# The second layer's bias of a two-layer MLP: from four small matrix products a window to one VectorE addition a pair of tiles, with a new order of the steady group

## The chip, the cores and the metric

The kernel runs on one core of one Trainium2 chip. A core has five engines that run their own instruction streams side by side and wait for each other by semaphores: TensorE (PE in the profile; its weight loads are listed as PEld), VectorE (DVE), ScalarE (ACT), GpSimd (POOL) and SyncE (SP, which here only issues DMAs). The metric is the device time of one execution in microseconds (us), as the median of several runs. Lower is better.

## The reference, cut to what matters

```python
def _mlp_ln(s, W1, b1, W2, b2, g, b):
    h = jax.nn.silu(s @ W1 + b1) @ W2 + b2
    return _ln(h, g, b)                          # (x - m) * rsqrt(v + EPS) * g + b
h = _ln(x, pw_g[pathway_ids], pw_b[pathway_ids])
h = _ln(h, cp_g[compartment_ids], cp_b[compartment_ids])
t = _ln(x, tm_g[time_steps], tm_b[time_steps])
m, n, r = x + (a normed MLP of a conditioning vector, one row a batch)   # three such
s = _ln(x, ms_g[scale_type], ms_b[scale_type])
cat = concatenate([w[0]*h, w[1]*t, w[2]*m, w[3]*n, w[4]*r, w[5]*s], axis=-1)
return x + _mlp_ln(cat, int_W1, int_b1, int_W2, int_b2, int_g, int_be)
```

x is 16 x 512 x 512 in float32, so there are 8192 tokens of 512 features. What is changed here is where `int_b2`, the bias of the second layer of the last MLP, is added.

## The kernel before, in words

**Tiling.** The 8192 tokens are walked in 16 windows of 512 tokens. A window is four tiles of 128 tokens (numbered 0 to 3), and two tiles make a pair (0 and 1 are pair 0, 2 and 3 are pair 1). Tokens are gathered by index from memory, so that a window shares its small tables.

**The order of the work** is written out by hand in three lists of short names: `ORDER` for the start, `WINDOW` for the steady group that is run once for each window (`run(WINDOW, w)`, L1408), and `LAST` for the last window. A name is a kind of step, a window and a number: `c` is the window at hand, `n` the next one, `m` the one after it, `p` the one before. Each engine runs its own steps in the order in which they stand in the list, so that the list fixes five queues at once. Pieces of three windows lie beside each other in one group.

**The steps that matter here**, with the lines under which the profile shows them:

- `lV` (layer1, L371): product of a tile's normed x with the window's own 512 x 512 matrix; four a window, 8 recorded matmuls each (a float32 matmul is recorded as two).
- `m7.c.p.k` (half_product, L419): two tiles' remaining first-layer products by seven products of half size (Strassen's scheme in Winograd's form), k from 1 to 7 for pair p, 8 recorded matmuls each. Sums of their inputs are made on VectorE: `u1` to `u4` (token_sum, L400, L402, L404, L406) write into the transposed tiles cX, cH and a tile ss. What comes out is added up on VectorE by `r1`, `r2`, `r3`, `r5` (L428 to L436) and `ha` (L439).
- `hs` (L442, ScalarE) is the SiLU, `tz` (L169, VectorE) turns a tile into rZ, and `sZ` (spread_row, L177) moves rZ to cZ by DMAs that SyncE issues, four for each of four rows. `tx`, `th`, `tv` and `sX`, `sH`, `sV` do the same for x, h and the normed x of the window. All these DMAs stand in SyncE's one queue.
- `zs` (z_sums, L499 to L505, GpSimd) makes the input sums of the second layer's seven products: `zs.p.0` to `zs.p.3` for pair 0, `zs.p.4` to `zs.p.7` for pair 1.
- `q7.p.q.k` (seventh, L522): the second layer of the window before, again as seven products for each pair q, 4 recorded matmuls each. They run in two banks of PSUM for a pair, called ab and ed (pq_0a, pq_0b, pq_1a, pq_1b in the profile).
- `kf`, `ku` (L531, L533, L544, ScalarE) copy from these banks to the result yb; `sf`, `sl` (L538, L540, L549, L551, VectorE) add what belongs to it. After `sl.p.1` both rows of tiles of pair 0 are finished, after `sl.p.3` those of pair 1.
- `lq` (L587, ScalarE) sums the squares of a finished tile, `lv` (L595) and `lp` (L600, GpSimd) make the inverse deviation, `lb` (L608, L609, VectorE) scales and adds x, `po` (L613, GpSimd) writes the tile out by an indirect DMA. `gx` gathers a later window's x into the buffer that this frees.
- `f1` (L314, L315), `f2` (L351), `fs`, `fv`, `fp`, `fn`, `th` are the chain of h; `bd` (L233) rebuilds a window's matrix where its group of tables changes, under a condition read from memory.

**The bias before.** `bias_parts` (L470) splits the row of b2 into three bfloat16 parts once, in b2r. In `seventh`, the products k = 1 and k = 5 are preceded by a small product of a constant with that row (L520, 96 rows x 256 columns in bfloat16), which starts the accumulation, so that the bias is in PSUM before the true product is added. All results that the seven products make up contain product 1 or 5 in the right way, so four small products a window do it. The first window and the last one go through `layer2` and `last_add` (L582), which add the row on VectorE.

Of the kernel before, what the change touches and what calls it, by code (L numbers as in the profile page):

```python
# [15 lines left out]
P = 128  # L16
# [9 lines left out]
WINDOW = """
    ha.p.2 lV.c.1 hs.p.2 sh.c.1 tz.p.3 gc.c.2 tz.p.2 sp.c.3 gc.c.3 f1.c.2 fs.c.2 f1.c.3 m7.c.1.1 m7.c.0.1 lV.c.0
    xs.n.0 fs.c.3 sh.c.0 bd.c.3 lV.c.3 fv.c.2 f2.c.2 f2.c.3 sZ.p.2 ga.c.0 sZ.p.0 xs.n.1 q7.p.1.1 fp.c.2 fv.c.3 fn.c.2
    q7.p.0.1 sZ.p.1 fp.c.3 q7.p.0.2 fn.c.3 sZ.p.3 sp.c.2 th.c.2 th.c.3 xs.n.2 zs.p.0 zs.p.1 bd.c.2 q7.p.0.5 kf.p.0
    q7.p.1.2 sH.c.0 sf.p.0 gh.n.0 zs.p.2 tx.n.3 kf.p.1 tx.n.0 q7.p.0.6 xs.n.3 zs.p.4 q7.p.0.7 ku.p.0 zs.p.5 q7.p.1.5  # L30
    zs.p.3 xe.n kf.p.2 tx.n.1 xp.n ga.c.1 sf.p.1 sH.c.3 tx.n.2 xm.n kf.p.3 q7.p.0.3 q7.p.1.7 sf.p.2 nv.n.3 q7.p.0.4
    sl.p.0 zs.p.6 nv.n.1 ga.c.2 zs.p.7 sh.c.3 tv.n.3 tv.n.1 r1.c.0 gc.n.0 sf.p.3 sl.p.1 nv.n.2 tv.n.2 m7.c.0.2 nv.n.0
    ga.c.3 sH.c.2 sH.c.1 lq.p.0 gh.n.1 tv.n.0 q7.p.1.3 lq.p.1 q7.p.1.6 ku.p.1 f1.n.0 q7.p.1.4 sl.p.2 fs.n.0 sl.p.3
    lV.c.2 lq.p.2 u1.c.0 u1.c.1 lq.p.3 va.n u3.c.0 sV.n.0 sV.n.3 u2.c.0 lv.p m7.c.0.4 r1.c.1 m7.c.0.5 lp.p m7.c.1.5
    u2.c.1 fv.n.0 lb.p.1 lb.p.0 vd.n r5.c.0 gc.n.1 u4.c.0 m7.c.0.6 u3.c.1 r5.c.1 gx.m.1 lb.p.2 sp.n.1 po.p.0 r2.c.0
    sV.n.2 f1.n.1 fp.n.0 m7.c.1.6 sV.n.1 sX.n.2 sX.n.0 m7.c.0.7 gx.m.2 sX.n.3 fs.n.1 sp.n.0 r2.c.1 f2.n.0 lb.p.3
    po.p.1 fv.n.1 gx.m.0 gx.m.3 fn.n.0 po.p.2 fp.n.1 bd.n.0 bd.n.1 f2.n.1 m7.c.1.7 m7.c.1.2 fn.n.1 u4.c.1 m7.c.0.3
    r3.c.0 th.n.0 gh.n.2 sh.c.2 ha.c.0 ha.c.1 r3.c.1 hs.c.1 m7.c.1.4 th.n.1 gh.n.3 hs.c.0 tz.c.1 ha.c.3 hs.c.3 po.p.3
    tz.c.0 sX.n.1 m7.c.1.3
"""  # L40

LAST = """
# [16 lines left out]
def kernel(ctx: ExitStack, tc: tile.TileContext, a: dict, out: bass.AP):  # L59
# [24 lines left out]
    nc = tc.nc  # L84
    B, S, D = a["x"].shape
# [40 lines left out]
    yb = const.tile([P, NJ, D], F32, name="yb")  # L126
    rows = const.tile([P, 3, D], F32, name="rows")
# [385 lines left out]
    def seventh(st, p, k):  # L513
        ab, ed = sums_of(st, p)
        home = {1: ab[:, 0], 6: ab[:, 0], 2: ab[:, 1], 5: ed[:, 0], 3: ed[:, 0], 7: ed[:, 1], 4: ed[:, 1]}[k]
        if ("zp", p) not in st:
            st["zp", p] = {1: st["cZ"][:, 2 * p, :2], 2: st["cZ"][:, 2 * p, 2:]}
        bias = at_["bias"]
        if k in bias:
            nc.tensor.matmul(home, at_["share"], bias[k], start=True, stop=False, skip_group_check=True)  # L520
        for c in range(2):
            nc.tensor.matmul(home, st["zp", p][k][:, c], at_["half"][k][:, c], start=False, stop=(c == 1),  # L522
                             skip_group_check=True)
# [22 lines left out]
    def sum_last(st, i):  # L546
        y, ab, ed = y_halves(st, i // 2)
        if i % 2 == 0:
            nc.vector.tensor_add(y[:, 3], y[:, 3], y[:, 2])  # L549
# [114 lines left out]
    for nm in ("mem", "noi", "res"):  # L664
        k = a[nm + "T"].shape[0]
# [115 lines left out]
    ex = prep.tile([P, 6], F32, name="ex")  # L781
# [40 lines left out]
    rc = prep.tile([P, 2, NQ], I32, name="rc")  # L822
# [51 lines left out]
    half = prep.tile([P, 2], F32, name="half")[:NB]  # L874
# [96 lines left out]
    both = prep.tile([P, NJ, NW], I32, name="both")  # L971
# [29 lines left out]
    at_ = {}  # L1001
# [400 lines left out]
    k = min(names.index(n) if n in names else len(names) for n in ("wq", "wz"))  # L1402
# [61 lines left out]
```

## Time and profile before

| | before |
|---|---|
| median of 3 runs | 945.38 us (942.22 to 946.45) |
| the profiled execution's own time | 937.16 us |
| its span, first to last instruction | 935.4 us |
| TensorE busy | 912.2 us |
| VectorE busy | 744.1 us |
| ScalarE busy | 500.8 us |
| GpSimd busy | 644.7 us |
| small products of the bias (L520) | 56, of 0.275 us each as recorded |
| VectorE additions L549 and L551 (`sl`) | 28 of each |

How to read it: matmuls overlap in their pipeline, so that a recorded 0.275 us is longer than the time from its start to the next one's start. What a product takes from TensorE is read from starts. An engine's busy time is no cost of its own where another engine ends later; the question at each step is which wait ends last. The profiled execution is one of the quick ones: its own time lies 8.2 us under the median of the runs.

### The profile page before, as it was taken

The page shows a single profiled execution, that of the slowest core. Times are in us where ns is not written, and L with a number is a line of the kernel's source. Part 1 is how long each engine was busy: PE and PEld are TensorE (multiplying, and loading weights), DVE is VectorE, ACT ScalarE, POOL GpSimd, SP SyncE. Part 2 cuts the span into 40 slices and gives each one's busy share as a digit, 9 for nine tenths or more (in the row PEclk, how much of TensorE's full clock was granted, in tenths as well). Part 3 has the DMA queues.
Part 4 walks back from the last instruction along what each step waited for, and adds up shares of the span by engine and source line. Part 5 has one row for each costly group of instructions (what it writes and reads, how often), then busy time and mean ns, then how long its engine had stood idle before and what let it go on. Part 6 is the DMA issues. An engine that isn't in the chain of part 4 may idle for free. (4 is left out here: it accounts for less than half of the span.)

```text
span 935.4 us, 13570 instructions
## 1 busy us (share of the span) xinstructions
PE 912.2 (98%) x3693; PEld 645.0 (69%) x3693; DVE 744.1 (80%) x1355; ACT 500.8 (54%) x1205; POOL 644.7 (69%) x697
## 2 busy tenths in 40 slices
PE   7999999999999999999999999999999999999996
PEld 6634444677768786868677787868686877767673
DVE  8558577877979698979788786969798988989475
ACT  5457853556372737554554727374656566473322
POOL 9455756657777777677787677777777778775533
PEclk9899999999999999999999999999999999999998
DMA  8756776786868777677868686776767786856613
GB/s 282 217 202 193 212 214 172 206 237 164 250 168 232 198 205 213 182 215 203 236 169 251 169 238 178 229 203 202 214 195 215 199 238 166 251 162 186 173 47 101
DMA packets 88861, 186.68 MB, mean 200 GB/s; under 512 B 24372, under 2 KB 24372, under 8 KB 88780
## 3 DMA queue, kind: packets, MB, share of 16 engines
q0 software_dynamic: 31376, 106.19, 40.2%
q1 hardware_dynamic: 56700, 79.50, 28.9%
q8 instruction: 31, 0.51, 0.2%
q14 instruction: 50, 0.41, 0.2%
q10 hardware_dynamic: 704, 0.08, 0.1%
HBM read 101.78 MB, written 19.94 MB: 130 GB/s over the span
## 5 line engine op out<-in xcount | busy, mean ns | idle before, releaser
L371 PE MATMUL p<-vs,cV 128*128 128x512 f32 x496 | 221.2, 593 | 1.5 <-ACT junk L318 0.7
L371 PEld LDWEIGHTS p<-vs,cV 128*128 128x128 f32 x496 | 93.8, 190 | 103.2 <-issue 78.8
L318 ACT ACTIVATE junk<-pw 128x512 bf16<-128x512 f32 x60 | 37.8, 629 | 170.4 <-DVE pw L315 160.0
L419 PE MATMUL p<-wh__80,cH 128*128 128x256 f32 x464 | 107.5, 379 | 0.0
L143 POOL DMA_INDIRECT xbs<-in_x,tok x64 | 69.4, 1085 | 46.5 <-DVE yb L609 22.8
L419 PEld LDWEIGHTS p<-wh__80,cH 128*128 128x128 f32 x464 | 88.2, 190 | 12.0
L613 POOL DMA_INDIRECT out<-yb,tok x64 | 65.6, 1025 | 42.9 <-issue 25.7
L143 POOL DMA_INDIRECT pw<-in_pw,i_pw x64 | 65.0, 1015 | 40.4 <-DVE rH L169 18.3
L143 POOL DMA_INDIRECT cp<-cp_rows,i_cp x64 | 78.0, 1219 | 20.1 <-issue 13.0
L359 POOL TENSOR_TENSOR xbs<-xbs,rows 128x512 f32<-128x512 f32 x64 | 82.7, 1293 | 1.1
L340 POOL TENSOR_TENSOR rsh<-veh,mhalf 128x1 f32<-128x1 f32 x64 | 47.9, 748 | 42.2 <-DVE veh L336 37.5
L143 POOL DMA_INDIRECT add<-rows,i_add x64 | 66.5, 1038 | 15.1 <-issue 14.8
L314 DVE SCALAR_TENSOR_TENSOR pw<-xbs,sums,pw 128x512 f32<-128x512 f32 x60 | 59.5, 992 | 21.3 <-DMA pw<-in_pw,i_pw 20.7
L344 ACT ACTIVATE pw<-pw,rsh 128x512 f32<-128x512 f32 x64 | 44.9, 716 | 55.6 <-POOL rsh L340 47.5
L442 ACT ACTIVATE add<-add 128x512 f32<-128x512 f32 x64 | 38.7, 626 | 63.1 <-DVE add L439 61.8
L419 PE MATMUL p<-wt,cH 128*128 128x256 f32 x240 | 56.7, 379 | 0.0
L419 PE MATMUL u<-wx__79,ss 128*128 128x256 f32 x240 | 54.7, 380 | 1.9 <-DVE ss L400 1.7
L351 DVE SCALAR_TENSOR_TENSOR pw<-pw,sumsh,cp 128x512 f32<-128x512 f32 x60 | 44.6, 748 | 14.9 <-ACT junk L320 7.0
L169 DVE STREAM_TRANSPOSE rH<-pw 128x512 f32<-128x512 f32 x60 | 41.2, 700 | 18.8 <-ACT pw L344 18.0
L587 ACT ACTIVATE junk<-yb 128x512 bf16<-128x512 f32 x64 | 40.3, 630 | 28.1 <-DVE yb L582 13.9
L419 PE MATMUL u<-wt,cX 128*128 128x256 f32 x240 | 54.3, 379 | 0.0
L419 PEld LDWEIGHTS u<-wx__79,cX 128*128 128x128 f32 x240 | 45.6, 190 | 12.6 <-issue 3.8
(437 smaller groups left out, 2130.9 us busy)
## 6 DMA issues: line engine op xcount, KB each, us to landing
cZ<-rZ SPq DMA_DIRECT2D x256, 64.0 KB
cV<-rV SPq DMA_DIRECT2D x240, 64.0 KB
cX<-rX SPq DMA_DIRECT2D x240, 64.0 KB
cH<-rH SPq DMA_DIRECT2D x240, 64.0 KB
w1x<-in_int_W SPq DMA_DIRECT2D x2, 1024.0 KB
rows<-adde SPq DMA_DIRECT2D x14, 128.0 KB
yb<-in_int_W SPq DMA_DIRECT2D x1, 1024.0 KB
ws<-in_int_W SPq DMA_DIRECT2D x1, 1024.0 KB
```

What stands on the lines that cost most here:

```text
L143: nc.gpsimd.indirect_dma_start(dst, None, table, bass.IndirectOffsetOnAxis(ap=idx, axis=0), **kw)
L169: nc.vector.transpose(rot[:, :, :, j, :].rearrange("p q c t -> p c q t"), src.rearrange("p (c q t) -> p c q t", c=NC, q=Q))
L314: nc.vector.scalar_tensor_tensor(h, st["xb"][:, j, :], st["sums"][:, 1, j : j + 1], h, ALU.add, ALU.mult)
L340: nc.gpsimd.tensor_tensor(rs, st.pop(("ve", j)), mhalf[:, :1], ALU.pow)
L344: nc.scalar.mul(pw[:, :D], pw[:, :D], st.pop(("rs", j)))
L351: nc.vector.scalar_tensor_tensor(pw[:, :D], pw[:, :D], st["sh", j][:, 1], cp, ALU.add, ALU.mult)
L359: nc.gpsimd.tensor_add(st["xb"][:, j, :], st["xb"][:, j, :], rows[:, 2, :])
L371: nc.tensor.matmul(st["p1", g], st["c" + blk][:, g, c, :], m[:, c, :], start=(blk == first and c == 0), stop=(blk == last and c == NC - 1) ...
L419: nc.tensor.matmul(dst, m[:, c], at_["half1"][k][:, c], start=(k == 1 and c == 0), stop=(c == NC - 1), skip_group_check=True)
L442: nc.scalar.activation(st["add", g], st["add", g], AF.Silu)
L587: nc.scalar.activation(junk, yb[:, j, :], AF.Square, accum_out=st["ssy"][:, j : j + 1])
L613: nc.gpsimd.indirect_dma_start(out_rows[j], bass.IndirectOffsetOnAxis(ap=tok[:, j, w : w + 1], axis=0), yb[:, j, :], None)
```

## The change

The small products go from `seventh`; the true products 1 and 5 start the accumulation now. Behind the last `sl` step of each pair (i = 1 and i = 3) VectorE adds the row of b2, float32, to both finished tiles of that pair in one instruction of 128 partitions x 1024 elements, in place. `bias_parts` still runs. `ORDER` is the same list with other line breaks; `LAST` is unchanged. `WINDOW` has the same 189 names in another order.

```diff
-        bias = at_["bias"]
-        if k in bias:
-            nc.tensor.matmul(home, at_["share"], bias[k], start=True, stop=False, skip_group_check=True)
         for c in range(2):
-            nc.tensor.matmul(home, st["zp", p][k][:, c], at_["half"][k][:, c], start=False, stop=(c == 1),
-                             skip_group_check=True)
+            nc.tensor.matmul(home, st["zp", p][k][:, c], at_["half"][k][:, c], start=(k in (1, 5) and c == 0),
+                             stop=(c == 1), skip_group_check=True)
...
             nc.vector.tensor_add(y[:, 1:3], y[:, 2:3].to_broadcast([P, 2, D // 2]), ed)
+            both = yb[:, 2 * (i // 2) : 2 * (i // 2) + 2]
+            nc.vector.tensor_add(both, both, rows[:, :1].to_broadcast([P, 2, D]))
```

The new `WINDOW` in the list's own order:

```diff
 WINDOW = """
...
+    vd.n ha.p.2 sh.c.0 lV.c.1 hs.p.2 tz.p.3 tz.p.2 lV.c.0 m7.c.0.1 sp.c.3 sZ.p.1 f1.c.2 bd.c.3 sp.c.2 m7.c.1.1 sZ.p.0
+    sh.c.1 lV.c.3 ga.c.0 gc.c.2 f1.c.3 fs.c.2 gc.c.3 xs.n.0 fv.c.2 sZ.p.2 fs.c.3 fp.c.2 q7.p.0.1 q7.p.0.2 xs.n.1
+    bd.c.2 fv.c.3 sZ.p.3 f2.c.2 fp.c.3 zs.p.0 va.n zs.p.1 fn.c.2 f2.c.3 q7.p.0.5 fn.c.3 zs.p.2 tx.n.0 q7.p.1.1 xs.n.2
+    th.c.2 kf.p.0 th.c.3 sf.p.0 kf.p.1 tx.n.1 xs.n.3 zs.p.3 gh.n.0 q7.p.1.2 q7.p.0.6 sH.c.0 zs.p.4 xe.n q7.p.0.7
+    ku.p.0 zs.p.5 sH.c.1 sf.p.1 xp.n tx.n.3 q7.p.1.5 q7.p.0.3 sl.p.0 xm.n ga.c.3 tx.n.2 kf.p.2 kf.p.3 zs.p.6 ga.c.1
+    sf.p.2 q7.p.1.7 r1.c.0 sf.p.3 nv.n.3 nv.n.1 tv.n.3 tv.n.1 q7.p.0.4 zs.p.7 nv.n.2 sl.p.1 ga.c.2 q7.p.1.6 nv.n.0
+    lq.p.0 sH.c.2 lq.p.1 tv.n.2 m7.c.0.2 gc.n.0 f1.n.0 q7.p.1.3 ku.p.1 sl.p.2 sH.c.3 q7.p.1.4 tv.n.0 sl.p.3 u1.c.0
+    m7.c.0.4 sV.n.3 u1.c.1 sV.n.0 fs.n.0 sV.n.1 lq.p.2 gh.n.1 lV.c.2 lq.p.3 u3.c.0 m7.c.0.5 sV.n.2 lv.p lp.p r1.c.1
+    m7.c.1.5 fv.n.0 u2.c.1 sX.n.2 u2.c.0 lb.p.1 gc.n.1 r5.c.0 lb.p.0 m7.c.1.2 sp.n.1 r5.c.1 u4.c.0 m7.c.0.6 m7.c.1.6
+    f1.n.1 fs.n.1 po.p.1 gx.m.1 r2.c.0 lb.p.2 gx.m.0 m7.c.0.7 u3.c.1 po.p.0 r2.c.1 fp.n.0 fv.n.1 po.p.2 fp.n.1
+    m7.c.1.7 lb.p.3 f2.n.0 m7.c.0.3 gx.m.2 sX.n.0 u4.c.1 m7.c.1.4 f2.n.1 m7.c.1.3 fn.n.0 th.n.0 bd.n.1 gx.m.3 r3.c.1
+    sX.n.3 sX.n.1 gh.n.2 sp.n.0 po.p.3 bd.n.0 fn.n.1 r3.c.0 sh.c.3 ha.c.1 sh.c.2 hs.c.1 th.n.1 ha.c.0 hs.c.0 ha.c.3
+    tz.c.1 hs.c.3 gh.n.3 tz.c.0
```

Engine by engine, the queues that the prediction speaks of read like this, before (b) and after (a):

```
TensorE b  lV.1 m7.1.1 m7.0.1 lV.0 lV.3 | q7: 1.1 0.1 0.2 0.5 1.2 0.6 0.7 1.5 0.3 1.7 0.4 (m7.0.2) 1.3 1.6 1.4
           | lV.2 m7: 0.4 0.5 1.5 0.6 1.6 0.7 1.7 1.2 0.3 1.4 1.3
TensorE a  lV.1 lV.0 m7.0.1 m7.1.1 lV.3 | q7: 0.1 0.2 0.5 1.1 1.2 0.6 0.7 1.5 0.3 1.7 0.4 1.6 (m7.0.2) 1.3 1.4
           | m7.0.4 lV.2 m7: 0.5 1.5 1.2 0.6 1.6 0.7 1.7 0.3 1.4 1.3
VectorE b  sf.1 tx.2 xm sf.2 sl.0 tv.3 tv.1 r1.0 sf.3 sl.1 tv.2 tv.0 f1.n.0 sl.2 sl.3 u1.0 u1.1 u3.0 u2.0 lv r1.1
           u2.1 fv lb.1 lb.0 vd r5.0 u4.0 u3.1 r5.1 lb.2 r2.0 f1.n.1 r2.1 ...
VectorE a  sf.1 tx.3 sl.0 xm tx.2 sf.2 r1.0 sf.3 tv.3 tv.1 sl.1 + bias tv.2 f1.n.0 sl.2 tv.0 sl.3 + bias u1.0 u1.1
           u3.0 lv r1.1 fv u2.1 u2.0 lb.1 r5.0 lb.0 r5.1 u4.0 f1.n.1 r2.0 lb.2 u3.1 r2.1 ...
SyncE   b  sZ: 2 0 1 3, sH: 0 3 2 1, sV: 0 3 2 1, sX: 2 0 3 1
SyncE   a  sZ: 1 0 2 3, sH: 0 1 2 3, sV: 3 0 1 2, sX: 2 0 3 1
```

More of the change, by code (lines that the diff above doesn't have):

```diff
@@ new lines @@
+    f1.0.2 vt.0.0 gx.e1.0 wk.2.2 wu.ex.4.1 fn.0.0 gr.e0.0 vt.0.3 wk.2.1 xv.0.2 cm vt.0.1 cr ht.0.0 rp.1 fs.0.2 f2.0.2
+    xs.e0.3 gh.0.1 fv.0.2 rp.0 xe.e0 wu.lX.0.1.7 hv.0.0 xp.e0 xm.e0 wl.4 vt.0.2 vv.0.3 nv.e0.0 vv.0.1 fp.0.2 rc.1
+    xs.e1.1 mt.e0.0 ar f1.0.1 rc.0 fn.0.2 gc.0.1 nv.e0.1 ro.1 sp.0.1 fs.0.1 lX.0.0 ey.0 ht.0.2 vd.0 f2.0.1 gr.e0.1
+    vv.0.2 fv.0.1 lX.0.3 gh.0.3 xs.e1.0 xa gr.e0.2 mt.e0.1 xs.e1.2 ez.0 hv.0.2 lX.0.1 gx.1.0 gx.1.1 wu.ex.0.0 nv.e0.2
+    fp.0.1 ey.1 nv.e0.3 ex.0 ro.0 bd.0.1 fn.0.1 ez.1 ea.0 sp.0.0 gr.e0.3 ht.0.1 gx.1.2 xe.e1 xp.e1 f1.0.3 fs.0.3
@@ L29 @@
[L29 to L38, printed above, removed]
```

22 lines of the change are left out of this document (18 added, 4 removed).

## The prediction, made before the changed kernel was run

> **What bounds the kernel now.** The page first, for the engine that is hardly ever idle.
>
> ```profile
> PE 912.2 (98%) x3693; PEld 645.0 (69%) x3693; DVE 744.1 (80%) x1355; ACT 500.8 (54%) x1205; POOL 644.7 (69%) x697
> ```
>
> Then the view of windows for the steady part, cut at the first small product of each window (212.59 is the first, 823.63 the thirteenth), and the waits of TensorE in that part. Columns of the first: length, then the busy time of each engine.
>
> ```profile
> 263.21:313.83 50.62, 50.62 (x205) 38.07 (x204) 40.18 (x74) 26.75 (x67) 37.36 (x38) 1.00 0.74 206
> 364.61:417.16 52.55, 50.99 (x206) 37.67 (x205) 47.52 (x80) 30.11 (x73) 38.77 (x38) 1.00 0.71 200
> 212.59:823.63 611.04, 608.64 (x2449) 455.94 (x2448) 511.17 (x904) 337.76 (x820) 455.84 (x457) 1.00 0.73 207
> ```
> ```profile
> PE pq_0a L522 <- DVE yb L538: 1.4, 1, 1.4
> PE p L371 <- ACT junk L318: 0.7, 1, 0.7
> ```
>
> An undisturbed window takes 50.62 us and TensorE has work for all of it, at the full clock (1.00). Twelve windows take 611.04, so 611.04 - 12 x 50.62 = 3.6 us go to windows in which VectorE rebuilds a matrix (47.52 us busy instead of 40.18). TensorE sets the pace, and whatever shortens its queue shortens the window, as long as all that it waits for still comes in time. Next, what it does in a window, from starts to starts.
>
> ```profile
> 518.62 0.28 PE L520 MATMUL pq_1a<-b2r,ident 96*128 96x256 bf16 x1
> 518.73 1.03 PE L522 MATMUL pq_1a<-w,cZ 128*128 128x256 f32 x4
> 519.60 0.28 PE L520 MATMUL pq_0a<-b2r,ident 96*128 96x256 bf16 x1
> ...
> 524.14 1.03 PE L522 MATMUL pq_0b<-w2t,yb 128*128 128x256 f32 x4
> 525.01 0.27 PE L520 MATMUL pq_1b<-b2r,ident 96*128 96x256 bf16 x1
> 525.21 1.10 PE L522 MATMUL pq_1b<-w,cZ 128*128 128x256 f32 x4
> 526.15 1.03 PE L522 MATMUL pq_0b<-w,yb 128*128 128x256 f32 x4
> ...
> 533.05 3.60 PE L371 MATMUL p<-vs,cV 128*128 128x512 f32 x8
> 536.49 1.89 PE L419 MATMUL p<-wt,cH 128*128 128x256 f32 x8
> 538.22 3.62 PE L419 MATMUL u<-wx__79,ss 128*128 128x256 f32 x16
> ```
>
> A second-layer product (q7) holds TensorE 0.87 us (518.73 to 519.60), a V product (lV) 3.44, a first-layer half product (m7) 1.73. A small product of the bias holds it 0.11 (518.62 to 518.73), recorded 0.28 or not.
>
> **Step 1: the small products go.** Three of a window's four cost 0.11. The fourth costs more: 525.01 to 526.15 is 1.14, against 0.87 (524.14 to 525.01) without it, so 0.27. Together 3 x 0.11 + 0.27 = 0.60 us a window. Thirteen windows from 212.59 on carry them inside the steady run: 13 x 0.60 = 7.8. The last window's own four lie partly in its waits; I take 0.2. Gain if nothing else came late: **8.0 us**.
>
> **Step 2: VectorE gets 28 additions** of 128 x 1024. The trace has that form only at the start, and the neighbours in VectorE's queue tell how long an operation holds it.
>
> ```profile
> L387 DVE TENSOR_TENSOR wx__79<-wx__79 x1: 1227/1227/1227, 149.0 to 149.0; 128x1024 f32<-128x1024 f32 x1
> ```
> ```profile
> 525.43 0.38 DVE L540 TENSOR_TENSOR yb<-yb,pq_0b 128x256 f32<-128x256 f32 x1
> ...
> 526.72 0.85 DVE L549 TENSOR_TENSOR yb<-yb 128x256 f32<-128x256 f32 x1
> ...
> 537.67 0.75 DVE L608 SCALAR_TENSOR_TENSOR yb<-yb,rsy,rows 128x512 f32<-128x512 f32 x1 [0.18 <-POOL rsy L600]
> 538.45 0.69 DVE L609 TENSOR_TENSOR yb<-yb,xbs 128x512 f32<-128x512 f32 x1
> 539.06 0.74 DVE L608 SCALAR_TENSOR_TENSOR yb<-yb,rsy,rows 128x512 f32<-128x512 f32 x1
> ...
> 540.45 0.41 DVE L432 TENSOR_TENSOR add<-add,u 128x256 f32<-128x256 f32 x1
> 540.78 0.41 DVE L433 TENSOR_TENSOR add<-add,u 128x256 f32<-128x256 f32 x1
> 541.11 0.69 DVE L406 TENSOR_TENSOR cH<-cH,ss 128x512 f32<-128x512 f32 x1
> 541.71 0.69 DVE L404 TENSOR_TENSOR cX<-cX 128x512 f32<-128x512 f32 x1
> ```
>
> A recorded 0.69 holds the queue 0.61 (538.45 to 539.06), so 1.23 holds it 1.15; an operation on what the one before just wrote starts 0.1 later (538.45 behind 537.67 is 0.78 for a recorded 0.75). That makes 1.25 each, 2.5 a window, 28 x 1.25 = 35 us in all. VectorE's 40.18 in an undisturbed window becomes 42.7 of 50: as a sum it lies beside TensorE. What counts is who stands behind the additions in VectorE's queue. ScalarE's squares lq wait for them, and behind lq in ScalarE's queue the copy ku.1, and for it sl.2; on VectorE itself stand u1, u2, the steps lb, and u3.1, without which TensorE can't start product 7 of pair 1.
>
> **Step 3: VectorE's stretch from sf.1 to u3.1.** Before, it runs from 525.43 to 541.71 + 0.69 = 542.40, so 16.97 us, and u3.1 is ready long ahead of its product. In the new order there stand in it besides: the two additions 2.5, a turn 0.61 (tx.3; 0.69-long like L609), r5.1 2 x 0.33 (540.45 to 540.78), r2.0 0.33, lb.2 1.39 (537.67 to 539.06), and f1 of the next window's tile 1, two operations like L608, 1.45. Sum 6.94; vd, which leaves it, reads a register and is taken at nothing. That is 23.9 us. Two things may go: the 0.18 of waiting at lb, and 0.44 in L549, recorded 0.85, not 0.41 like L432 of the same size, while it ran beside this one:
>
> ```profile
> 527.25 0.91 POOL L503 TENSOR_TENSOR zs<-cZ 128x256 f32<-128x256 f32 x1
> ```
>
> In the new order sl.0 stands where GpSimd makes a power and gathers. So 23.3 to 23.9. TensorE goes from the end of q7.0.7, which lets sf.1 start, to product 7 of pair 1 over 7 second-layer products (1.5, 0.3, 1.7, 0.4, 1.6, 1.3, 1.4), 8 half products and one V product: 7 x 0.87 + 8 x 1.73 + 3.44 = 23.37, and sf.1 starts some 0.3 after that end (525.43 is 0.42 behind 525.01). There are 23.07 us for 23.3 to 23.9 of work: TensorE waits 0.2 to 0.8 a window. Below that end I put 0, since pieces may overlap by a tenth each. I take 0.2: the hold by GpSimd has lost its partner.
>
> **Step 4: SyncE's queue.** Its order is a part of the change, and every window issues 64 DMAs there.
>
> ```profile
> 509.04 10.30 SPq L177 DMA_DIRECT2D cZ<-rZ  x16
> ...
> 548.77 11.29 SPq L177 DMA_DIRECT2D cX<-rX  x16
> 560.17 1.80 SPq L177 DMA_DIRECT2D cZ<-rZ  x3
> ```
> ```profile
> 518.74 0.74 POOL L499 TENSOR_TENSOR yb<-cZ 128x256 f32<-128x256 f32 x1 [1.89 <-DMA cZ<-rZ]
> ```
>
> The cX DMAs start when the last reader of the old cX is through: m7.1.7 ends at 538.22 + 6 x 1.73 = 548.6, and 0.2 later they go. cZ follows at once (560.17). The third of its four rows is issued by 509.04 + 0.75 x 10.30 = 516.77, and zs.0, which waited for it, starts 1.97 later. Now product 2 of pair 1 is taken ahead of the products 6, so that m7.1.7 ends 1.73 nearer to the next window's q7. Path of the data: 0.2 + 11.40 (548.77 to 560.17) + 10.30 + 1.97 + two sums of 0.74 (zs.4, zs.5) = 25.35 us from m7.1.7 to product 5 of pair 1. Path of TensorE: three m7, three V, two m7, seven q7: 5 x 1.73 + 3 x 3.44 + 7 x 0.87 = 25.06. Before, TensorE's path was 1.73 longer and the data had slack. Now the wait is 0 to 0.3 a window; I take 0.15, since the quoted cX block is a long one. All DMAs behind (sH, sV) still start after their own producers.
>
> **Step 5: windows with a rebuild** cost 3.6 now. The rebuild ahead of sf.0 should stop holding TensorE (the 1.4 above): product 6 of pair 0 has one more product ahead of it. The rebuilds late in the window push the last turns and so cZ, which has no slack now. Between -1.4 and +3; I take +0.5.
>
> **Step 6: the end.** After the last pair VectorE waits for TensorE.
>
> ```profile
> 917.35 0.69 DVE L582 TENSOR_TENSOR yb<-p,rows 128x512 f32<-128x512 f32 x1 [2.75 <-PE p L454]
> ```
>
> The addition of 1.25 fits into that gap of 2.75. Without the gap it would cost 1.25; I take 0.
>
> **The sum**, against the profiled execution (937.16 us, of which 935.4 are the span): -8.0 + 13 x (0.2 + 0.15) + 0.5 = -2.95, so 934.2. The three timed runs' median lies 8.2 higher for the same kernel; I carry the difference over: 945.38 - 2.95 = **942.4 us**, -0.3%. About 0.5%, 4.7 us, is what a measurement of this kernel can tell from no change, so the forecast is no change by that bound. Its own range goes from 940.7 to 947.
>
> **Rivals.**
>
> *The order fits, and the whole gain stays.* For it: in the old order TensorE waits nowhere in an undisturbed window, although things come in time by a hair there too. Against it: both paths above come out longer than TensorE's. It gives 945.38 - 8.0 = 937.4 us; with the 1.4 of the rebuild 936.0.
>
> *VectorE's stretch becomes the bound.* Mechanism: additions with both inputs in SBUF are held while GpSimd adds, as L549 is beside L503 (0.85 instead of 0.41). In the new order zs.7 runs close to the first addition. If one such hold of 0.44 stays in the stretch and the wait at lb as well, u3.1 is 0.8 late: a window costs 50.62 - 0.60 + 0.8 + 0.15 = 50.97, 13 x 0.35 = 4.6 more, with the rebuilds at +1.5 a sum of 945.38 + 4.6 + 1.5 - 0.2 = 951.3 us. It decides from a lateness of 0.60 - 0.15 = 0.45 us a window.
>
> Beside this rival stands a rule of the Trainium skill, "SBUF — State Buffer", section "Who interferes with whom": a VectorE instruction with two SBUF inputs and a GpSimd instruction that reads SBUF exclude each other for the whole of the one that came first. The trace agrees where L549 meets L503; by that rule a held addition would lose up to the whole GpSimd operation, and each of the 28 is open to it.
>
> **How the numbers follow.** Forecast (no change) 0.42, all of the gain 0.33, the stretch 0.25. The forecast's own range reaches a little beyond the bound on the fast side, which gives faster 0.35, same 0.40, slower 0.25. The range holds both rivals: from 936.5, just inside the full gain, to 951.5.
>
> **What would show it.** No L520 rows, and the steps from product to product at 0.87 throughout: step 1. L551 followed by a 128x1024 row of 1.23: step 2; longer ones of up to 2: the second rival. Waits of PE u L419 on DVE cX L404: step 3. Waits of PE pq_1b on POOL cZ L501, with cZ's DMAs starting less than 9 us ahead of the first q7: step 4. A window of 50.0 shows the first rival right, one of 50.97 the second. The prediction is wrong at its base if TensorE's steps don't shrink by 0.60, or if another queue, SyncE's or GpSimd's, stretches the window.

## The result, and the profile after

The changed kernel takes 966.86 us (median of four runs, 963.01 to 970.78), the kernel before 943.8 us (median of four). The ratio is 1.0265, with a 95% interval of 1.0223 to 1.0308: slower by about 25 us, where no change had been forecast and 951.5 us was the end of the range. The profiled execution of the changed kernel took 969.87 us, that of the kernel before 937.16. One execution of e9 (2460.51 us) and one of e12 (5441.43 us) were far slower than all others and are left out of the times given below.

The old kernel's lines ahead of the product q7 stand 22 further down in the new one (L419 is L441, L501 is L523), q7 (L522) is L541, the lines from there to the new addition stand 19 further down, and the addition is L572. First the page, for the engines as before:

```profile
PE 920.5 (95%) x3637; PEld 643.2 (66%) x3637; DVE 771.7 (80%) x1383; ACT 499.7 (52%) x1205; POOL 656.9 (68%) x697
```

TensorE is idle for 5% of the span now, not 2%, though it has 56 small products less to do. The view of windows, cut at the first product q7 of each window (the last row holds twelve windows, as the row 212.59:823.63 of before did):

```profile
270.44:323.45 53.01, 52.46 (x200) 38.79 (x201) 42.40 (x73) 25.14 (x62) 37.40 (x37) 0.97 0.68 195
430.92:484.36 53.44, 50.95 (x200) 37.58 (x201) 43.23 (x76) 27.06 (x69) 38.18 (x38) 1.00 0.69 197
217.33:856.34 639.01, 614.04 (x2401) 453.53 (x2400) 535.37 (x927) 336.67 (x820) 466.67 (x455) 0.99 0.70 198
```

Twelve windows take 639.01 us and took 611.04: 28.0 us more, 2.3 a window. The rest of the difference between the two profiled executions (4.7) lies ahead of the first of these windows, where both run the same list: there TensorE's granted clock stood at 0.50 for 17.1 us in this execution (38.65 to 55.71) and for 10.2 in the one of before (39.03 to 49.27). What TensorE waited for in the steady part:

```profile
PE pq_0a L541 <- DMA cZ<-rZ: 17.6, 12, 2.4
PE pq_0b L541 <- POOL cZ L523: 4.2, 5, 1.3
PE u L441 <- DVE veh L358: 2.0, 6, 0.3
PE u L441 <- DVE add L452: 1.0, 3, 0.3
```

Before, this list came to 2.9 us. Now the first q7 of a window waits 12 times for the DMAs that bring cZ, the third (q7.0.5) five times for GpSimd's sum zs.1 behind it, and the product m7.1.7 nine times for VectorE. One window from the timeline, SyncE's DMAs first, then TensorE with one row of VectorE:

```profile
516.76 10.72 SPq L199 DMA_DIRECT2D cX<-rX  x16
527.81 10.51 SPq L199 DMA_DIRECT2D cZ<-rZ  x16
...
512.42 1.99 PE L441 MATMUL u<-wt,cX 128*128 128x256 f32 x8
514.74 1.99 PE L441 MATMUL u<-wt,cX 128*128 128x256 f32 x8 [0.33 <-DVE veh L358]
...
514.27 0.41 DVE L452 TENSOR_TENSOR add<-add,u 128x256 f32<-128x256 f32 x1
...
532.07 3.60 PE L393 MATMUL p<-vs,cV 128*128 128x512 f32 x8
536.50 1.97 PE L541 MATMUL pq_0a<-w,cZ 128*128 128x256 f32 x8 [0.83 <-DMA cZ<-rZ]
539.02 1.13 PE L541 MATMUL pq_0b<-w,cZ 128*128 128x256 f32 x4 [0.56 <-POOL cZ L523]
```

The first q7 reads row 0 of cZ, which SyncE sends second, by its DMAs 5 to 8. The eighth is issued by 527.81 + 8/16 x 10.51 = 533.07; the product starts 3.4 us later. The product m7.1.7 (514.74) starts 2.32 us behind m7.0.7 (512.42) instead of 1.73: it adds to what r2.1 (L452) has to read first, and r2.1 ends at 514.27 + 0.41 = 514.68. From starts to starts it is 0.59 late; the list gives 0.33, because recorded matmuls overlap. And the additions themselves:

```profile
L572 DVE TENSOR_TENSOR yb<-yb,rows x28: 1224/1226/1226, 229.1 to 947.3; 128x1024 f32<-128x1024 f32 x28
```

All 28 take what step 2 said. None is held.

So there were two theories. **Order**: the new `WINDOW` is slow by itself, because it brings the first product nearer to SyncE's chain. **Additions**: VectorE's stretch has no room for 2.5 us more, and all else follows from that.

### The profile page after: what moved, and what is told of

It reads as the page before. It is cut to its first block, busy times and chain, and to the rows that moved or that the text cites. A ratio compares the mean times of both kernels' runs of the same rounds, so it can differ in the third digit from the quotient of the medians.

```text
span 968.1 us, 13675 instructions
## 1 busy us (share of the span) xinstructions
PE 920.5 (95%) x3637; PEld 643.2 (66%) x3637; DVE 771.7 (80%) x1383; ACT 499.7 (52%) x1205; POOL 656.9 (68%) x697
## 5 line engine op out<-in xcount | busy, mean ns | idle before, releaser
L634 POOL DMA_INDIRECT out<-yb,tok x64 | 80.4, 1256 | 55.5 <-DVE add L455 17.1
L441 PE MATMUL p<-wh__80,cH 128*128 128x256 f32 x464 | 109.6, 379 | 0.0
L441 PEld LDWEIGHTS p<-wh__80,cH 128*128 128x128 f32 x464 | 88.2, 190 | 12.0
L362 POOL TENSOR_TENSOR rsh<-veh,mhalf 128x1 f32<-128x1 f32 x64 | 51.6, 806 | 53.1 <-DVE veh L358 44.2
L165 POOL DMA_INDIRECT cp<-cp_rows,i_cp x64 | 69.7, 1089 | 23.2 <-issue 16.7
L165 POOL DMA_INDIRECT pw<-in_pw,i_pw x64 | 62.5, 977 | 29.6 <-issue 12.3
L165 POOL DMA_INDIRECT add<-rows,i_add x64 | 70.8, 1106 | 13.1 <-issue 12.8
L336 DVE SCALAR_TENSOR_TENSOR pw<-xbs,sums,pw 128x512 f32<-128x512 f32 x60 | 57.4, 956 | 27.1 <-DMA pw<-in_pw,i_pw 22.7
L621 POOL TENSOR_TENSOR rsy<-vey,mhalf 128x4 f32<-128x4 f32 (+1 forms) x16 | 16.5, 1030 | 70.8 <-DVE vey L616 70.8
L441 PE MATMUL u<-wt,cX 128*128 128x256 f32 x240 | 58.8, 389 | 3.8 <-DVE veh L358 2.0
L307 ACT ACTIVATE xm<-xbs,nmx,rsx 128x512 f32<-128x512 f32 x64 | 49.0, 807 | 23.3 <-DVE nmx L301 6.6
L441 PE MATMUL p<-wt,cH 128*128 128x256 f32 x240 | 56.7, 379 | 0.0
L441 PE MATMUL u<-wx__79,ss 128*128 128x256 f32 x240 | 54.5, 380 | 1.6 <-DVE ss L422 1.4
L441 PE MATMUL u<-wt,ss 128*128 128x256 f32 x240 | 54.5, 379 | 1.2 <-DVE add L455 1.2
```

Source lines behind the costliest of these rows:

```text
L165: nc.gpsimd.indirect_dma_start(dst, None, table, bass.IndirectOffsetOnAxis(ap=idx, axis=0), **kw)
L307: nc.scalar.activation(t, st["xb"][:, j, :], AF.Identity, bias=st["nm"][:, j : j + 1], scale=st["rs"][:, j : j + 1])
L336: nc.vector.scalar_tensor_tensor(h, st["xb"][:, j, :], st["sums"][:, 1, j : j + 1], h, ALU.add, ALU.mult)
L362: nc.gpsimd.tensor_tensor(rs, st.pop(("ve", j)), mhalf[:, :1], ALU.pow)
L441: nc.tensor.matmul(dst, m[:, c], at_["half1"][k][:, c], start=(k == 1 and c == 0), stop=(c == NC - 1), skip_group_check=True)
L634: nc.gpsimd.indirect_dma_start(out_rows[j], bass.IndirectOffsetOnAxis(ap=tok[:, j, w : w + 1], axis=0), yb[:, j, :], None)
```

## The experiments

Ratios are to the kernel before in the same set of runs, with 95% intervals. The sets ran on different chips, so ratios are what is compared between them. A per cent is 9.4 us.

### e1 to e4: order and additions taken apart

`e1_old_order` is the changed kernel with the old list:

```diff
 WINDOW = """
-    vd.n ha.p.2 sh.c.0 lV.c.1 hs.p.2 tz.p.3 tz.p.2 lV.c.0 m7.c.0.1 sp.c.3 sZ.p.1 f1.c.2 bd.c.3 sp.c.2 m7.c.1.1 sZ.p.0
+    ha.p.2 lV.c.1 hs.p.2 sh.c.1 tz.p.3 gc.c.2 tz.p.2 sp.c.3 gc.c.3 f1.c.2 fs.c.2 f1.c.3 m7.c.1.1 m7.c.0.1 lV.c.0
...
```

`e2_new_order_products` is the old kernel with the new list. `e3_new_order_no_bias` is the changed kernel and `e4_old_order_no_bias` is e1, each without this line, so the bias is missing in their output:

```diff
-            nc.vector.tensor_add(both, both, rows[:, :1].to_broadcast([P, 2, D]))
```

> The bias is added by VectorE as in the changed kernel, but the steady group keeps the order that it had before. Theory 'order' (the 26 us of waits after the change come from where the new order puts the products and the hidden-row steps, above all that the first product of a group now waits for the DMAs of cZ): no such waits here, so the old period of 50.62 us loses up to the 0.60 us of the small products: 936 to 942 us, below the kernel before by 1 to 8 us. Rival 'additions' (28 additions of 1.23 us fill VectorE, and the waits come from VectorE and SyncE being late behind them): 955 to 967 us, most of the loss is here too.

> The new order of the steady group, with the bias still by small products on TensorE as before; VectorE has no additions. Theory 'order': the waits of the changed kernel are here too; the small products cost 8 us but part of them runs while TensorE waits for cZ anyway: 964 to 972 us. Rival 'additions': without the additions the order is harmless: 940 to 948 us.

> The changed kernel with the second layer's bias left out altogether (no additions on VectorE, no products on TensorE; the output lacks the bias). Theory 'order': almost the changed kernel's time, 958 to 966 us, because SyncE's chain from the last reader of cX to the landing of cZ stays. Rival 'additions': 936 to 942 us.

> The kernel before with the second layer's bias left out altogether (the output lacks the bias): what the removal of the products is worth in the old order with nothing put in its place. Both theories: 935 to 938 us, period 50.0 us, if nothing else takes the 0.6 us of a window; 941 to 944 if SyncE's chain (25.35 against 25.06 us) eats it.

| bias | old order | new order |
|---|---|---|
| small products | 1 | e2: 1.0149 (1.0093 to 1.0205) |
| none | e4: 0.9954 (0.9926 to 0.9983) | e3: 1.0156 (1.0098 to 1.0213) |
| additions on VectorE | e1: 1.0532 (1.0485 to 1.0578) | the change: 1.0265 (1.0223 to 1.0308) |

Neither theory stands alone: e1 (988.24 us) lies above both of its ranges, e2 (952.21) and e3 (951.77) lie between theirs, and e4 (934.37) is just under the lower one. Without any bias the new order costs 2.0% (e3 less e4, 19 us). In the old order the additions cost 5.8% (e1 less e4, 54 us), in the new one 1.1% (10 us; the 15 in the expectation of e12 was a difference of medians from two sets of runs). Leaving the small products out is worth 0.46% in the old order (4.3 us, not 8.0) and nothing in the new one (e2 and e3 agree). Put in a row, the change is -0.46 + 2.0 + 1.1 = 2.65%; this adds up by construction. By the intervals each of these differences can be off by 0.3 to 0.7.

The windows say the same. Twelve of them in e1, e3 and e4, in this order, and one undisturbed window of e4:

```profile
213.66:870.63 656.97, 623.22 (x2402) 457.58 (x2401) 554.80 (x929) 337.22 (x821) 461.34 (x457) 0.98 0.68 193
```
```profile
209.39:834.04 624.65, 609.63 (x2402) 454.98 (x2400) 507.95 (x904) 334.94 (x817) 458.76 (x456) 0.99 0.72 203
```
```profile
264.31:314.47 50.16, 50.16 (x202) 37.83 (x200) 40.26 (x74) 26.72 (x66) 37.35 (x38) 1.00 0.74 209
213.76:820.65 606.89, 604.76 (x2401) 452.59 (x2400) 508.06 (x904) 338.06 (x820) 454.23 (x457) 1.00 0.73 209
```

The undisturbed window falls from 50.62 to 50.16, by 0.46 and not by 0.60: four times 0.11. TensorE's waits in e1, then in e3:

```profile
PE u L441 <- DVE add L455: 30.9, 13, 2.4
```
```profile
PE pq_0a L541 <- DMA cZ<-rZ: 12.2, 9, 2.2
PE pq_0b L541 <- POOL cZ L523: 2.4, 3, 1.6
PE u L441 <- DVE veh L358: 0.3, 1, 0.3
```

In the old order TensorE waits for r5 (L455) on VectorE in every window, 2.4 us, and never for cZ's DMAs. In the new order it waits for them with the additions or without (8.3 us in e2). The new order takes away most of what VectorE's additions hold TensorE for and pays with SyncE's chain. What is left of it shows from starts to starts: over the thirteen windows from the first q7 on, the products 7 start 8.6 us later in the changed kernel than steps of 1.73 would have it, and 0.9 in e3, where most windows have no gap between them:

```profile
291.85 3.62 PE L441 MATMUL u<-wt,cX 128*128 128x256 f32 x16
```

So 7.7 us of what the additions cost in the new order are this wait, and the waits for cZ are longer with them too (17.6 us against 12.2 in the lists).

And e1 shows a thing that the changed kernel doesn't; VectorE first, then GpSimd:

```profile
499.58 2.31 DVE L572 TENSOR_TENSOR yb<-yb,rows 128x1024 f32<-128x1024 f32 x1
...
505.70 1.22 DVE L572 TENSOR_TENSOR yb<-yb,rows 128x1024 f32<-128x1024 f32 x1
...
499.52 1.27 POOL L381 TENSOR_TENSOR xbs<-xbs,rows 128x512 f32<-128x512 f32 x1
```

The first addition of a window takes 2.31 us beside GpSimd's addition of 1.27 us (step `sh.c.3`), the second 1.22 alone: VectorE loses 1.09, nearly the whole of GpSimd's operation; 12 of the 14 first additions take 2.3 to 2.4. This is the mechanism of the second rival, in the order in which the change was not made.

### e5 and e6: what GpSimd has to do with it

In e5 the shift goes away from the addition; in e6 GpSimd makes the additions.

```diff
-    sl.p.0 zs.p.6 nv.n.1 ga.c.2 zs.p.7 sh.c.3 tv.n.3 ... r3.c.0 th.n.0 gh.n.2 sh.c.2 ha.c.0
+    sl.p.0 zs.p.6 nv.n.1 ga.c.2 zs.p.7 tv.n.3 ... r3.c.0 th.n.0 gh.n.2 sh.c.2 sh.c.3 ha.c.0
```
```diff
-            nc.vector.tensor_add(both, both, rows[:, :1].to_broadcast([P, 2, D]))
+            nc.gpsimd.tensor_add(both, both, rows[:, :1].to_broadcast([P, 2, D]))
```

> As e1 (additions on VectorE, old order), but GpSimd's shift of the third tile's rows, a 1.2 us tensor addition that in e1 lay beside the first addition of each window, is moved to the other shift near the window's end. In e1 that addition took 2.31 us, the other one 1.23. Theory 'held by GpSimd' (VectorE stands still while GpSimd adds, and the stretch has no slack, so 1.08 us a window comes off TensorE's wait of 2.54 us, and half-pace products after the wait become fewer): 958 to 975 us against 988. Rival 'stretch alone' (the wait is the 2.5 us of additions in a full stretch, the held time was hidden): 984 to 990 us.

> As e1, but the 28 bias additions are made by GpSimd, at the same place of the order. Theory 'VectorE's instruction count' (only work in VectorE's own queue counts): 936 to 946 us. Rival 'shared' (a tensor addition on GpSimd, some 2.5 us for 1024 columns by the 1.28 us of its additions of 512, stops VectorE's two-input operations meanwhile): 965 to 1000 us, no better than e1.

e5: 972.98 us, 1.0360 (1.0310 to 1.0410), 1.7% or 16 us below e1. "Held by GpSimd" is right. e6: 1031.6 us, 1.0991 (1.0947 to 1.1035): "shared" is right, and worse than the 1000 us at which its range ended. The waits of e5, then in e6 the additions and two of VectorE's, of which one runs beside an addition:

```profile
PE u L441 <- DVE add L455: 23.7, 13, 1.9
```
```profile
L572 POOL TENSOR_TENSOR yb<-yb,rows x28: 2346/2364/2664, 225.8 to 1005.7; 128x1024 f32<-128x1024 f32 x28
```
```profile
287.63 3.44 DVE L422 TENSOR_TENSOR ss<-cX,cH 128x512 f32<-128x512 f32 x2
```

In e5 the wait for r5 is 1.9 us still: VectorE works almost without a gap from sl to there, and 2.5 us of additions that nobody holds make TensorE wait 2. On GpSimd an addition takes 2.36 us, nearly twice as long, its followers start later, and VectorE's u1 (L422), 0.68 us by itself in e1, is held beside it: the two of the row take 3.44.

### e7 to e9: what the wait for cZ hangs on

e7 is e3 with one block of TensorE's, product 2 of pair 1, back where the old order has it:

```diff
-    m7.c.1.5 ... m7.c.1.2 sp.n.1 r5.c.1 u4.c.0 m7.c.0.6 m7.c.1.6 ... m7.c.1.7 lb.p.3
+    m7.c.1.5 ... sp.n.1 r5.c.1 u4.c.0 m7.c.0.6 m7.c.1.6 ... m7.c.1.7 m7.c.1.2 lb.p.3
```

> As e3 (new order, bias left out, so its output lacks the bias), with one product block of 1.73 us, m7 of pair 1 number 2, moved back behind m7 of pair 1 number 7, the last reader of cX. Theory 'SyncE's chain' (last reader of cX, 16 DMAs of cX, DMAs of cZ, landing, first product of the second layer sets the period in the new order): the chain starts 1.73 us earlier while TensorE's own work until the first product stays the same, so most of the 12 us of waits for cZ goes: 937 to 943 us against 951.8. Rival 'traffic' (cZ's DMAs land late whatever their start, because other transfers fill the DMA engines): 948 to 953 us.

959.42 us, 1.0211 (1.0158 to 1.0265): no better than e3 (the 0.55% above it are not clear of the noise), and outside both theories' numbers. The waits tell why:

```profile
PE pq_0a L541 <- DMA cZ<-rZ: 5.8, 4, 3.3
PE pq_0b L541 <- POOL cZ L523: 3.5, 8, 0.6
PE u L441 <- issue: 3.1, 9, 0.4
PE u L441 <- DVE add L452: 3.1, 10, 0.3
PE u L441 <- DVE add L455: 1.6, 3, 0.8
```

The wait for cZ falls from 12.2 us in nine windows to 5.8 in four, 3.3 of it in one: SyncE's chain does start too late for the first q7 in the new order. But the block had also given VectorE 1.73 us, and without it the products that use what VectorE makes wait for r2 and r5, even with no additions. The block is lent to one wait or to the other.

e8 takes VectorE out of the way in the changed kernel (u3.1 ahead of r5.0, lb.2 behind r2.1). e9 sends row 0 of cZ ahead of row 1.

```diff
-    ... u2.c.1 sX.n.2 u2.c.0 lb.p.1 ... r2.c.0 lb.p.2 gx.m.0 m7.c.0.7 u3.c.1 po.p.0 r2.c.1
+    ... u2.c.1 sX.n.2 u2.c.0 u3.c.1 lb.p.1 ... r2.c.0 gx.m.0 m7.c.0.7 po.p.0 r2.c.1 lb.p.2
```
```diff
-    ... sp.c.3 sZ.p.1 f1.c.2 bd.c.3 sp.c.2 m7.c.1.1 sZ.p.0
+    ... sp.c.3 sZ.p.0 f1.c.2 bd.c.3 sp.c.2 m7.c.1.1 sZ.p.1
```

> The changed kernel, with VectorE's step u3 of pair 1 moved ahead of r5 of pair 0 and its step lb of tile 2 moved behind r2 of pair 1, so that the two operations no longer stand between r2 of pair 0 and r2 of pair 1, for which the last products before the chain wait. Theory 'VectorE late feeds the chain': the 0.5 to 0.9 us that these products wait in each window go, and the waits for cZ shrink as the chain no longer starts later than TensorE: 950 to 960 us against 966.9. Rival 'landing alone': 963 to 968 us, the wait moves from u to cZ.

> The changed kernel with two steps of SyncE's queue exchanged: the four DMAs of cZ's row 0, which the first product of the second layer reads, go ahead of those of row 1. Theory 'first row lands late' (the 17.6 us that this product waits for cZ's DMAs are the loss): its wait goes, as row 0 is issued 2.5 us earlier (four DMAs at 0.63 us), and with it 12 to 16 us: 951 to 956 us. Rival 'next in line' (GpSimd's two sums of rows 0 and 1, which the third product needs, start when both rows are there, and TensorE has only 1.7 us of products ahead of them): the wait moves from the first product to the third, 962 to 968 us.

e8: 964.75 us, 1.0278 (1.0237 to 1.0319), the same as the change. e9: 964.14 us (median of three), 1.0349 (1.0288 to 1.0410), no better. The waits of e8 and then of e9:

```profile
PE pq_0a L541 <- DMA cZ<-rZ: 18.1, 12, 2.1
PE pq_0b L541 <- POOL cZ L523: 3.5, 5, 1.5
PE u L441 <- DVE pw L337: 0.8, 2, 0.4
```
```profile
PE pq_0b L541 <- POOL cZ L523: 19.1, 10, 2.2
PE pq_0b L541 <- DMA cZ<-rZ: 4.5, 2, 2.3
```

With VectorE early (e8) its waits halve (from 3.2 to 1.5 us in the lists) and the wait for cZ stays, 18.1 us where the change has 17.6. It could not shrink: TensorE's way to the first q7 and SyncE's chain both start at the end of m7.1.7, and a late m7.1.7 moves both. With row 0 early (e9), the first two q7 start in time and the third waits for zs.1, which needs both rows: "next in line". What sets the end is the landing of the second of these two rows.

### e10 to e14: is there room for the additions anywhere

VectorE is idle for nearly half of the time between its last turn to rZ and some 5 us after the first q7. e10, e11 and e13 take the old order with the additions (as e5) and move there the last operations on two of the four finished tiles (lb, 1.4 us each), with their output po and the gather gx into their rows. e12 is e11 without a bias, e14 is e13 with the small products. `LAST` gets the moved steps too, and from e11 on the next window's rows are summed (xs) in the order in which they now arrive.

```diff
# e10
+    tz.p.2 lb.o.2 po.o.2 gx.n.2 lb.o.3 po.o.3 gx.n.3 sp.c.3 gc.c.3 f1.c.2 ...
# e11
+    f1.c.3 lb.o.0 po.o.0 gx.n.0 m7.c.1.1 ... fp.c.2 fv.c.3 lb.o.1 ... fp.c.3 po.o.1 ... zs.p.0 zs.p.1 gx.n.1
# e13
+    fp.c.2 fv.c.3 lb.o.0 ... fp.c.3 po.o.0 ... th.c.3 lb.o.1 zs.p.0 zs.p.1 po.o.1 gx.n.0 gx.n.1 ... zs.p.2
```

(`o` is the window ahead of `p`.)

> As e5 (bias by VectorE, old order, GpSimd's shift out of the way), with VectorE's last operations on the finished rows (two for each tile, 1.4 us a tile) moved out of its full stretch: tiles 1 and 0 take the places of tiles 2 and 3, and tiles 2 and 3, with their output and the gather into their rows, go behind the last transposition of the hidden rows, where VectorE is idle a third to half of the time. Theory 'full stretch' (in the old order the whole loss is that VectorE's run of work without a gap got 2.5 us longer): 2.8 us are taken out ahead of the point where TensorE waits 2.0 us, so that wait goes and nothing else is late: 936 to 944 us against 973. Rival 'the sum counts' (VectorE is too full over the whole window, the wait turns up at another product or at the transpositions): 955 to 970 us.

> As e5 (bias by VectorE, old order, GpSimd's shift out of the way), with VectorE's last operations on tiles 0 and 1 (1.4 us a tile), their output and the gather into their rows moved out of the full stretch into the next window, behind the second front step and behind the second variance, where VectorE waits for ScalarE; tiles 2 and 3, whose rows GpSimd's sums use as space, stay where they were, so that no sum waits for an output as in e10. Theory 'full stretch': 2.8 us less ahead of the product that waited 2.0 us, nothing else late: 936 to 944 us. Rival 'the sum counts': the time turns up again, at GpSimd's sums or at the hidden rows: 955 to 990 us.

> As e11 with the bias left out (the output lacks the bias): what the additions cost where the stretch has room for them, beside 53.9 us between e1 and e4 in the old order and 15.1 us between the changed kernel and e3. Theory 'full stretch': e11 and e12 within 3 us of each other, both 934 to 944 us. Rival 'the sum counts': e12 lower than e11 by over 10 us.

> As e11, but the two moved tiles' last operations stand around the transpositions of the hidden rows, where VectorE is idle for 1.5 and 4 us, their outputs are put behind GpSimd's power and behind its first two sums (in e11 an output stood in GpSimd's queue ahead of the power and the sums and held both), and ScalarE's sums of the rows that are gathered late come last. Theory 'full stretch': neither VectorE nor GpSimd is late, 936 to 946 us. Rival 'no room' (any place for 2.9 us of VectorE costs another engine's wait): 955 us or more.

> The order of e13 with the bias by small products on TensorE as before: what the change is worth in an order that has room for the additions. Theory 'full stretch': e13 lower by up to the 4 us that leaving the products out gave in the old order. Rival 'no room': e13 higher by 10 us or more.

| | us | ratio (95%) |
|---|---|---|
| e10 | 992.84 | 1.0608 (1.0560 to 1.0655) |
| e11, additions | 1004.74 | 1.0721 (1.0683 to 1.0758) |
| e12, no bias (median of three) | 1001.92 | 1.0758 (1.0692 to 1.0825) |
| e13, additions | 1036.29 | 1.1055 (1.0996 to 1.1114) |
| e14, products | 1039.77 | 1.1106 (1.1049 to 1.1164) |

The times of e10, e11 and e13 are on the side of their rivals ("the sum counts", "no room"); e10 and e11 lie even above the rivals' ranges. In e12 and e14 the rivals are wrong: e12 is not 10 us below e11, nor e13 10 us above e14. These pairs can't be told apart, so in these two orders the additions cost nothing that can be measured, with room for some 4 us in the intervals. The waits for VectorE's r5 are gone, and a queue that I had not counted takes their place (35.6 us in e10 at the same product). TensorE's waits of e11, then of e12, then GpSimd in e13:

```profile
PE pq_0b L541 <- POOL cZ L523: 30.7, 12, 3.4
PE pq_0a L541 <- POOL yb L525: 10.8, 10, 2.0
```
```profile
PE pq_0b L541 <- POOL cZ L523: 31.3, 12, 3.2
```
```profile
564.71 1.05 POOL L523 TENSOR_TENSOR cZ<-cZ 128x256 f32<-128x256 f32 x1
565.93 1.01 POOL L634 DMA_INDIRECT out<-yb,tok  x1 [0.16 <-issue]
567.24 1.00 POOL L165 DMA_INDIRECT xbs<-in_x,tok  x1 [0.30 <-issue]
...
570.77 0.74 POOL L525 TENSOR_TENSOR yb<-cZ 128x256 f32<-128x256 f32 x1
```

Moving lb moves outputs and gathers, some 1.0 us each in GpSimd's queue, ahead of the sums for which TensorE waits: in e13 zs.2 starts 5 us behind the end of zs.1. So these five don't show an order in which room for the additions is free. Nor do they show that it is the room that makes the additions cost nothing here: TensorE waits for GpSimd up to 3.4 us in a window of e11, and 2.5 us of additions may as well lie hidden behind that.

### e15 and e16: the one block in the old order

e15 is e5 with product 2 of pair 1 where the new order has it, everything else old. e16 also brings the turns of x (tx) forward.

```diff
-    gc.n.1 u4.c.0 m7.c.0.6 ... m7.c.1.7 m7.c.1.2 fn.n.1
+    gc.n.1 u4.c.0 m7.c.1.2 m7.c.0.6 ... m7.c.1.7 fn.n.1
```
```diff
-    th.c.2 th.c.3 xs.n.2 zs.p.0 ... sf.p.0 gh.n.0 zs.p.2 tx.n.3 kf.p.1 tx.n.0 ... tx.n.1 ... tx.n.2
+    th.c.2 th.c.3 tx.n.3 tx.n.0 xs.n.2 zs.p.0 ... sf.p.0 tx.n.1 tx.n.2 gh.n.0 zs.p.2 kf.p.1 ...
```

> As e5 (bias by VectorE, old order, GpSimd's shift out of the way), with the one block of 1.73 us, m7 of pair 1 number 2, moved ahead of m7 of pair 0 number 6, where the new order has it. Theory 'trade' (the block gives VectorE 1.73 us at the point where TensorE waited 2.0 us, and starts SyncE's chain 1.73 us later against the first product that reads row 0, for which the old order, with row 2 and its product first, still has some 1.2 us): the wait for VectorE falls to 0.3 us, one for cZ of some 0.5 us comes: 948 to 958 us against 973, below the changed kernel's 967 and above the kernel before. Rival 'no trade' (the waits for cZ come to as much as in the new order, 1.5 us and more a window): 962 to 972 us.

> As e15, and VectorE's four transpositions of the rows x (0.65 us each) ahead of the places where they were, two of them at once behind the hidden rows' transpositions, where VectorE is idle for 1.5 us. Theory 'stretch': what is left of the wait for VectorE goes (0.3 us a window), nothing else moves: 944 to 955 us, up to 5 us below e15. Rival 'bounded by the product': the stretch begins where TensorE's products of the second layer end, so work taken out ahead of it frees nothing: within 3 us of e15.

e15: 963.25 us, 1.0281 (1.0210 to 1.0351); e16: 967.27 us, 1.0308 (1.0264 to 1.0352). By its time e15 falls into the rival's range (962 to 972), level with the change; by the ratios it is 0.8% below e5 (7.4 us), just not clear of the noise. Its waits:

```profile
PE pq_0b L541 <- POOL cZ L523: 6.6, 8, 1.7
PE pq_0a L541 <- DVE yb L557: 3.0, 1, 3.0
PE p L441 <- DVE cH L428: 2.8, 3, 1.0
PE p L393 <- DVE vs L255: 1.6, 2, 1.3
...
PE u L441 <- DVE add L455: 1.5, 9, 0.2
```

The block alone takes the wait for r5 from 23.7 to 1.5 us. What comes for it is not the 1.5 us a window for cZ of the rival but the 0.5 of the theory (6.6 us at the sums of cZ) and many small waits besides, at the V products above all; together they eat half of the gain. e16 is no better than e15 (0.3% above it, within the noise), as its rival had it ("bounded by the product"). No run of the change, with whatever order, comes below the kernel before; only e4, without the bias, does.

## Why the prediction was wrong, step by step

**Step 1** (8.0 us for the small products) is mis-sized. e4 gains 0.46% (4.3 us), and its undisturbed window 0.46 us. Three of the small products were right at 0.11. The fourth, taken at 0.27 because the product behind it came late, is worth 0.46 - 0.33 = 0.13 by that, so nearly all of the late start (0.27 - 0.11 = 0.16) stays without it.

**Step 2** (1.23 us each, 28 times) is right: 1.226. In the old order the first one of nearly every window would have been 2.3 (e1).

**Step 3** (VectorE's stretch, 0.2 us of wait a window, 0 to 0.8) named the right stretch and ended it one operation too early: m7.1.7 waits for r2.1, which stands behind lb.2 and u3.1 in VectorE's queue and takes 0.33 more. No wait for u3.1 itself, the sign that the prediction named, is in the list. From starts to starts the products 7 are 8.6 us late, 0.66 a window, inside the step's 0 to 0.8 and three times the 0.2 that it took. The additions cost 10 us by the ratios (e3 to the change); why the waits for cZ grow with them as well is not shown.

**Step 4** (SyncE's queue, 0.15 us a window) is the step that failed. It followed the data to product 5 of pair 1 and did not ask for the first q7, which the new order makes the first reader of row 0, where before another q7 and its row stood ahead of it. To ask for it would not have been enough: with the step's own numbers the path to the first q7 is 0.2 + 11.40 + 5.15 (eight of sixteen issues) + 1.97 = 18.72, against 18.97 of TensorE, and no wait. The term that was too small is the landing, 1.97 us. It was one of several in the trace of before, where zs.0 starts 1.6 to 3.3 us behind the end of the twelfth issue in the windows in which it waits for it.

What the window shown has, from its first cX DMA: 11.05 to the first cZ DMA, 5.26 for eight issues, 3.43 to the product's start, 19.74 in all. TensorE's path is three m7, three lV and two m7, 18.97, less the 0.2 at the start: 18.8. The difference, 0.9, is the wait of that window (0.83 in its row). In the twelve windows that wait, the product starts 3.3 to 4.8 us behind the end of the eighth issue; this window has the shortest. Of the two signs that the prediction named for this step, cZ's DMAs start less than 9 us ahead of the first q7 (8.69), and product 5 doesn't wait. Before, the old place of the block and the q7 ahead gave TensorE 1.73 + 0.87 + 0.2 more, and the same chain was covered.

The step's 2 us for thirteen windows measure 19 (e3 less e4), of which e3's list has 14.6 as waits for cZ and for zs.1 behind it. That it is this chain, and not VectorE, rests on e7 to e9: with TensorE's way 1.73 longer the wait falls by half, with VectorE early it stays, with row 0 early it goes to the reader of the other row. What makes the landing long was not measured by itself.

**Step 5**: the wait of 1.4 us ahead of sf.0 did go (it is not in the list of waits any more), but the clock (below) was not thought of. **Step 6** was right: from the last window's first q7 to the end the kernel takes 60.3 us, against 60.8 before (968.1 - 907.8 and 935.4 - 874.6).

Of the **rivals**, the first (all of the gain stays) falls with step 4. The second was right in its mechanism and wrong in its place: in the new order no addition is held. In the old order e1 and e5 price it at 16 us, and e6 shows it with the engines exchanged. The rule of the Trainium skill that stood beside it, "SBUF — State Buffer", section "Who interferes with whom", agrees with the trace here: an operation with two SBUF inputs on VectorE lost 1.09 us beside an addition of 1.27 on GpSimd that had started first (e1).

## What to carry to other kernels

Work that "lies beside" the busiest engine is free only as long as the stretch of its own engine up to the next wait has room: 2.5 us a window cost 54 us in 13 windows of e1, where the stretch was full, and 10 in the changed kernel. When an order moves a block, follow the data to the first reader of every row that it brings nearer, with the landing time of a row in the same busy stretch and not of the quietest one. And price an order and an edit separately before believing in either: here the order alone cost 14 us (e2), the edit alone 50 (e1), and both together 25.

## What the runs showed of the hardware that was not expected

**The clock falls after short waits, sometimes.** Two stretches of the changed kernel, each a wait of TensorE and what follows it (the last three columns are clock, DMA share and GB/s):

```profile
266.00:270.40 4.40, 2.47 (x6) 0.76 (x4) 1.05 (x3) 4.18 (x12) 1.27 (x2) 1.00 0.83 244
270.44:274.20 3.76, 3.76 (x10) 2.98 (x11) 2.28 (x4) 3.21 (x9) 3.02 (x5) 0.55 0.30 71
```
```profile
427.00:430.92 3.92, 2.20 (x7) 0.69 (x5) 1.09 (x3) 3.73 (x11) 0.98 (x1) 1.00 0.88 257
430.92:434.00 3.08, 3.08 (x13) 2.43 (x14) 2.28 (x4) 3.02 (x9) 2.51 (x4) 1.00 0.35 81
```

After 1.9 us of idle time (4.40 - 2.47) the granted clock is 0.55 as the mean of 3.76 us; after 1.7 us it stays at 1.00, and so it does after the longest wait of the list, 2.4 us (856.34 to 860.00). The changed kernel has two such stretches from the first q7 on, e1 seven, behind waits of 2.4 us. A window of e1 with one takes 55.04 us (213.66 to 268.70, clock 0.97) and one without 53.54 (488.49 to 542.03, clock 1.00), though TensorE waits 2.4 us in it too. By this 1.5 us, an estimate, the clock has some 10 of e1's 54 us. The change's four runs took 963.0 and 963.9 us at a mean clock of 0.994 and 0.993, and 969.9 and 970.8 us at 0.985 and 0.986. The Trainium skill, "TensorE: Matmul & The Clock Gate", section "What's actually happening", puts the drop to half behind an idle window of some 3.4 us whose phase runs freely. The trace agrees with a clock of about half and with its length, but shows it behind waits shorter than that.

**The same DMA lands after 1.97 us or after 3.4.** So much passed between the issue of a 64 KB move from rZ to cZ and the start of its reader, in step 4's row and in the window shown above. In the first stretch (516.77 to 518.74) the DMA engines were 48% busy, in the second (533.07 to 536.50) 80%; that this is the reason was not tested. The Trainium skill, "DMA: Bandwidth & Descriptors", section "Anatomy of one DMA — SWDGE (gpsimd) path", gives a fixed cost of about 2.0 us for another path; the first of the two is near it, the second is not.
